# State-space scales as 128 short rows, context scales kept on chip, biases as rows, and a second product buffer, in a decoder layer on one core

## The chip, the cores and the metric

The kernel runs on one core of a Trainium2 chip. The metric is device time in microseconds (us). Engines are named as in the profile: PE is TensorE's matmuls and PEld its weight loads, DVE is VectorE, ACT is ScalarE, POOL is GpSimd, SP is SyncE, and SPq its queue. Here SP issues all DMAs. L187 is line 187 of the kernel before.

## What is computed

The reference is one decoder layer on x (16 batches, 256 positions, 512 channels) with a context tensor of the same shape. Three sublayers each add to x:

```
x = x + attention(layernorm(x))                        # 16 heads of 32, causal
x = x + state_space(ctx, ctx, layernorm(x), kernel, D) # see below
x = x + ffn(layernorm(x))                              # int8-like rounding of x, h and both weights

# state_space: 32 heads; k = v = ctx, read as (batch, 256 rows, 512)
kv[i,j] = k[i] * v[j]                  # 8 x 8 products a head
y[i,j]  = causal convolution of kv[i,j] with the head's 512-tap kernel, plus D * kv[i,j]
out[j]  = sum over i of y[i,j] * q[i]
```

The ffn rounds rows to 127 steps of their largest magnitude, does silu(gate) * up, rounds again and multiplies by the down weights.

## The kernel before

It has two long stages. In the first (0 to about 694 us) attention runs over 64 units, each a batch and a group of four heads: `project` (q and k), `scores`, `flip` and `weigh` (weights times values), with `norm`, `turn`, `values` and `project_out` once a batch. The result x1 goes to device memory, `x1_d`.

Beside attention the first stage prepares the two later sublayers:

- `pairs` (L679) makes the 8 x 8 products of the context for each of 64 pieces (2 halves of the batches, 4 groups, 8 heads). `pairs_load` (L650) loads four context tiles `ct` and computes a power-of-two scale for each row in `sm`: its column 2 goes into the context, and its column 3 (L660) is stored in device memory, `rs_d` (L661), to undo it later. `pairs_turn` scales and transposes a tile to `kT`. `pairs` itself multiplies on POOL into a float32 tile `p` (L688, L692), copies it as f16 on ACT (L696), subtracts that copy from `p` on POOL for the f16 remainder (L697) and stores both parts in `kv_d` (L698). `p` has one buffer (L685), `kv` two.
- `state_space` (L701) scales the 32 convolution kernels by powers of two, stores the 32 inverse scales in `sg_d` (L713) and padded taps in `pad_d`.
- `wjob` and the weight functions behind it round the ffn weights to `w1_d` and `w2_d`, and their scales to `sw_d`.

`pairs` is spread over units 0 to 53 of the 64 (L858). Weight jobs are `pinned` (L789): on each engine they are tied behind the newest marked instruction, among them L697 and L698.

After unit 59, `side` is closed, the pools of `pairs` and the weights with it, and `conv_open` (L123) opens the convolution's tiles. It loads `sgt`, the scales as the convolution needs them: rows 0 to 63 hold the 16 scales of even heads and rows 64 to 127 those of odd ones (L128). Then come the first three `conv_load` (L176). Each loads a tile of 128 rows of x1 (`bx`, L178), every fourth also loads four row scales `rs` from `rs_d` (L181); row norms follow (L170 on ACT, L172 on DVE, L173 on POOL), then the factor of norm, row scale and kernel scale (L185, which needs `rs` and `sgt`), the scaled query (L187), its transposes on PE (L191) and copies (L192, L193). `conv_taps` loads the products `bkv` and the taps `T`.

The second stage runs over 32 tiles: `conv` multiplies taps and products on PE into `c` (L219 to L221), weighs with the query on DVE (L224 to L230), sums on POOL and DVE (L234 to L242); `conv_out` transposes back and adds x1, with `rs` as a factor (L250); the ffn follows some tiles later (`ffn_x`, `ffn_g`, `ffn_u`, `ffn_h`, `ffn_d`). `ffn_weights` loads its weights during the first tiles.

At the very start `bias_load` (L411) loads three bias vectors of 512 so that element 128c + p stands in row p, column c, four bytes at a time (L414), and takes their largest magnitude per row (L415), which `weight_scales` needs (L428).

Two things set the order of instructions on each engine. Each engine runs its own in order. That order is not the code's: when the kernel is built a planner (L921) lays the instructions out by its own model of times, starting what it believes ready, as far as data, free buffers and `pinned` allow. The code's order is a priority.

Of the kernel before, what the change touches and what calls it, by code (L numbers as in the profile page):

```python
# [8 lines left out]
F32 = mybir.dt.float32  # L9
# [3 lines left out]
I32 = mybir.dt.int32  # L13
AF = mybir.ActivationFunctionType
ALU = mybir.AluOpType
# [19 lines left out]
def kernel(  # L35
# [4 lines left out]
    nc = tc.nc  # L40
# [5 lines left out]
    CH = ssm.shape[0]  # L46
    HB = 8
    NHF = NB // HB
    NCG = 4
    NKV = 288  # L50

    P = 128
    KC = D // P
# [3 lines left out]
    cst = ctx.enter_context(tc.tile_pool(name="cst", bufs=1))  # L57

    def dtile(shape, dt, name):
        return dram.tile(shape, dt, tag=name, name=name)  # L60
# [2 lines left out]
    DX = D + 16  # L63
    x1_d = [dtile([HB, S, DX], F32, f"x1_d{f}") for f in range(NHF)]
    kv_d = [[dtile([P, 4, 2, NKV], F16, f"kv_d{f}_{h}") for h in range(CH)] for f in range(NHF)]
    rs_d = [[dtile([P, 4], F32, f"rs_d{f}_{c}") for c in range(NCG)] for f in range(NHF)]
    pad_d = dtile([CH, 2, 640], F16, "pad_d")
    sg_d = dtile([CH, 1], F32, "sg_d")
    NG, NW = 2 * I // P, 2 * I // P + D // P
# [5 lines left out]
    idf = cst.tile([P, P], F32, name="idf")  # L75
# [18 lines left out]
    def sd(nm):  # L94
        return ps_sd.tile([P, 512], F32, tag="sd", name=f"sd_{nm}")
# [14 lines left out]


    NK = 4 * NCG
    UW = 5 * 64 + 3 * 88
    cv = ff = tail = ps_c = ps_x = sgt = vs = sw1 = sw2 = w1 = w2 = None
    us = []
# [7 lines left out]
    def conv_open():  # L123
        nonlocal cv, sgt, vs
        cv = cv_ctx.enter_context(tc.tile_pool(name="cv", bufs=2, side="right", reuse_waits="tile"))
        sgt = cv.tile([P, NK], F32, bufs=1, name="sgt")
        for j in range(2):
            nc.sync.dma_start(  # L128
                sgt[64 * j:64 * j + 64, :], bass.AP(sg_d.tensor, sg_d.offset + j, [[0, 64], [2, NK], [1, 1]]))
        for j in range(2):  # L130
            products(cv)
        vs = cv.tile([P, 4, 88], F32, bufs=1, name="vsum")
# [28 lines left out]
            return ps_av.tile([P, 512], F32, tag="av", name=nm)  # L161
        return ps_pj.tile([P, 512], F32, tag="pj", name=nm)

    x1s, x2s, qTs, oTs, rss, kvT = {}, {}, {}, {}, {}, {}
    fst = {}


# [8 lines left out]
    def conv_load(f, k):  # L176
        x1 = cv.tile([P, DX], F32, tag="x1", bufs=5, name=f"bx1_{f}_{k}")
        nc.sync.dma_start(x1[:, :D + 1], rows(x1_d[f], 0, k, D + 1, DX))  # L178
        if k % 4 == 0:
            rss[f, k // 4] = cv.tile([P, 4], F32, tag="rs", bufs=3, name=f"rs{f}_{k}")  # L180
            nc.sync.dma_start(rss[f, k // 4], rs_d[f][k // 4])  # L181
        rs = rss[f, k // 4][:, k % 4:k % 4 + 1]
        q = cv.tile([P, D], F32, tag="q", bufs=2, name=f"bq{f}_{k}")
        st = row_norm(x1, q, f"b{f}_{k}")
        nc.vector.tensor_scalar(st[:, 2:3], st[:, 2:3], rs, sgt[:, k:k + 1], ALU.mult, ALU.mult)  # L185
        nc.vector.tensor_scalar(st[:, 3:4], x1[:, D:D + 1], st[:, 2:3], -1.0 / D, ALU.mult, ALU.mult)
        nc.scalar.activation(q, x1[:, :D], AF.Identity, bias=st[:, 3:4], scale=st[:, 2:3])  # L187
        qT = cv.tile([P, 2, 4, 96], F32, tag="qT", bufs=4, name=f"qT{f}_{k}")
        pt = sd(f"q{f}_{k}")
        for li in range(4):  # L190
            nc.tensor.transpose(pt[:, li * P:(li + 1) * P], q[:, li * P:(li + 1) * P], idf)  # L191
        nc.scalar.copy(ap(qT, 0, [[96, 4], [384, 2], [1, 64]]), pt.rearrange("p (l h i) -> p l h i", l=4, h=2))  # L192
        nc.scalar.copy(ap(qT, 64, [[96, 8], [1, 32]]), ap(qT, 0, [[96, 8], [1, 32]]))  # L193
        x1s[f, k], qTs[f, k] = x1, qT
# [47 lines left out]
            nc.vector.tensor_tensor(oT[:, :, 64 * h:64 * h + 64], a, vs[:, :, 0:64], ALU.add)  # L242

    def conv_out(f, k):
        x1, rs, oT = x1s[f, k], rss[f, k // 4][:, k % 4:k % 4 + 1], oTs[f, k]
        pt = sd(f"o{f}_{k}")
        for li in range(4):
            nc.tensor.transpose(pt[:, li * P:(li + 1) * P], oT[:, li, :], idf)
        x2 = ff.tile([P, DX], F32, tag="x2", bufs=DN + 4, name=f"x2_{f}_{k}")
        nc.vector.scalar_tensor_tensor(x2[:, :D], pt, rs, x1[:, :D], ALU.mult, ALU.add,  # L250
                                       accum_out=x2[:, D:D + 1])
        x2s[f, k] = x2

    OB, ND = 6, 2
    G, U, DN = 3, 4, 6
    end = f"{NHF - 1}_{NK - 1}"
    nt = {}
# [125 lines left out]
    with ExitStack() as ph:  # L383
# [7 lines left out]
        wld = wl_ctx.enter_context(tc.tile_pool(name="wld", bufs=1, side="right"))  # L391
# [8 lines left out]
        bias = wp.tile([P, 4, KC], F32, name="bias")  # L400
# [9 lines left out]

        def bias_load():  # L411
            nc.vector.memset(bias[:, 3, :], 0.0)
            for j, src in enumerate((q_b, k_b, v_b)):
                nc.sync.dma_start(bias[:, j, :], src.rearrange("(c p) -> p c", p=P))  # L414
            nc.vector.tensor_reduce(tbp, bias, op=ALU.max, axis=AX.X, apply_absolute_value=True)  # L415
            nc.vector.tensor_tensor(tbp, tbp, tbp, ALU.mult)

# [232 lines left out]
        def pairs_load(f, c):  # L650
            ct = kvp.tile([P, 4, D], F32, tag="ct", name=f"ct{f}_{c}")
            for k in range(4):
                nc.sync.dma_start(ct[:, k, :], rows(ctxt, f * HB, 4 * c + k))
            sm = kvp.tile([P, 4, 4], F32, tag="sm", bufs=2, name=f"sm{f}_{c}")
            nc.vector.tensor_reduce(sm[:, 0, :], ct, op=ALU.max, axis=AX.X, apply_absolute_value=True)
            nc.vector.tensor_scalar(sm[:, 0, :], sm[:, 0, :], 2.0 ** -100, None, ALU.max)
            si = sm.bitcast(I32)
            nc.vector.tensor_scalar(si[:, 1, :], si[:, 0, :], EXPMASK, None, ALU.bitwise_and)
            nc.vector.tensor_scalar(si[:, 2, :], si[:, 1, :], -1, (127 + 127 + 6) << 23, ALU.mult, ALU.add)
            nc.vector.tensor_scalar(si[:, 3, :], si[:, 1, :], 6 << 23, None, ALU.subtract)  # L660
            nc.sync.dma_start(rs_d[f][c], sm[:, 3, :])  # L661
            cts[f, c] = ct, sm

        def pairs_turn(f, c, k):
# [14 lines left out]
        def pairs(f, c, h):  # L679
                if h == 0:  # L680
                    pairs_load(f, c)
                if h % 2 == 0:
                    pairs_turn(f, c, h // 2)
                kT = kTs[f, c]
                p = kvp.tile([P, 4, NKV], F32, tag="p", bufs=1, name=f"p{f}_{c}_{h}")  # L685
                kv = kvp.tile([P, 4, 2, NKV], F16, tag="kv", bufs=2, name=f"kv{f}_{c}_{h}")
                o = (h % 2) * 384
                nc.gpsimd.tensor_tensor(  # L688
                    ap(p, 0, [[NKV, 4], [64, 4], [1, 64]]),
                    ap(kT, o, [[96, 4], [0, 4], [1, 64]]),  # L690
                    ap(kT, o, [[96, 4], [8, 4], [1, 64]]), ALU.mult)
                nc.gpsimd.tensor_tensor(  # L692
                    p[:, :, 256:NKV],
                    ap(kT, o, [[96, 4], [1, 32]]),
                    ap(kT, o + 32, [[96, 4], [1, 32]]), ALU.mult)
                nc.scalar.copy(kv[:, :, 0, :], p)  # L696
                marks["POOL"] = nc.gpsimd.tensor_tensor(kv[:, :, 1, :], p, kv[:, :, 0, :], ALU.subtract).ins  # L697
                marks["SP"] = nc.sync.dma_start(kv_d[f][8 * c + h], kv).ins  # L698


        def state_space():  # L701
            kr = ldp.tile([CH, 512], F32, tag="row", name="kr")
            kd = ldp.tile([CH, 4], F32, tag="kd", bufs=1, name="kd")
            nc.sync.dma_start(kr, ssm)
            nc.sync.dma_start(kd[:, 0:1], dskip.rearrange("(h o) -> h o", o=1))
            nc.vector.tensor_tensor(kr[:, 0:1], kr[:, 0:1], kd[:, 0:1], ALU.add)
            nc.vector.tensor_reduce(kd[:, 0:1], kr, op=ALU.max, axis=AX.X, apply_absolute_value=True)
            nc.vector.tensor_scalar(kd[:, 0:1], kd[:, 0:1], 2.0 ** -100, None, ALU.max)
            kdi = kd.bitcast(I32)
            nc.vector.tensor_scalar(kdi[:, 1:2], kdi[:, 0:1], EXPMASK, None, ALU.bitwise_and)  # L710
            nc.vector.tensor_scalar(kdi[:, 2:3], kdi[:, 1:2], -1, (127 + 127 + 14) << 23, ALU.mult, ALU.add)
            nc.vector.tensor_scalar(kdi[:, 3:4], kdi[:, 1:2], 14 << 23, None, ALU.subtract)
            nc.sync.dma_start(sg_d, kd[:, 3:4])  # L713
            nc.vector.tensor_scalar(kr, kr, kd[:, 2:3], None, ALU.mult)
            pad = ldp.tile([CH, 2, 640], F16, tag="row", name="pad")
            nc.vector.memset(pad, 0.0)
            nc.vector.tensor_copy(pad[:, 0, 127:639], kr)
            nc.vector.tensor_tensor(pad[:, 1, 127:639], kr, pad[:, 0, 127:639], ALU.subtract)
            nc.sync.dma_start(pad_d, pad)
# [206 lines left out]
```

## Time and profile before

| what | value |
|---|---|
| time, median of 3 runs (lowest to highest) | 1297.2 us (1295.33 to 1301.08) |
| the profiled execution: its time | 1293.03 us |
| its span, first to last instruction | 1290.9 us |
| mean granted TensorE clock | 0.950 of full |
| busy, share of the span | PE 87%, DVE 81%, POOL 73%, ACT 63% |

The profiled execution is 4.2 us under the median, so durations from the profile add up against 1293, and differences are then taken from 1297.2.

The page also cuts the span in 40 slices of 32 us. A digit is the busy share of a slice in tenths; PEclk is the granted clock in tenths; the last row is what the DMA engines moved:

```profile
PE   4889789998998989989993688999999899999985
...
PEclk8889889999998989989998889999999999999998
...
GB/s 237 111 143 201 178 190 212 205 207 214 173 238 183 217 187 201 253 178 206 231 178 73 377 178 161 173 155 158 160 158 176 149 157 153 177 144 161 128 70 74
```

PE is busy in nearly every slice. The two low digits in the middle (slices 22 and 23, counted from 1, 678 to 742 us) are the change from attention to convolution, and the DMA engines move only 73 GB/s in the first of them. Shares of busy time over the whole span say little about such a place, so the stage has to be looked at on its own.

### The profile page before, as it was taken

The page shows a single profiled execution, that of the slowest core. Times are in us where ns is not written, and L with a number is a line of the kernel's source. Part 1 is how long each engine was busy: PE and PEld are TensorE (multiplying, and loading weights), DVE is VectorE, ACT ScalarE, POOL GpSimd, SP SyncE. Part 2 cuts the span into 40 slices and gives each one's busy share as a digit, 9 for nine tenths or more (in the row PEclk, how much of TensorE's full clock was granted, in tenths as well). Part 3 has the DMA queues.
Part 4 walks back from the last instruction along what each step waited for, and adds up shares of the span by engine and source line. Part 5 has one row for each costly group of instructions (what it writes and reads, how often), then busy time and mean ns, then how long its engine had stood idle before and what let it go on. Part 6 is the DMA issues. An engine that isn't in the chain of part 4 may idle for free.

```text
span 1290.9 us, 25306 instructions
## 1 busy us (share of the span) xinstructions
PE 1127.8 (87%) x8487; PEld 775.5 (60%) x8487; DVE 1044.8 (81%) x3034; ACT 818.5 (63%) x1970; POOL 940.5 (73%) x882
## 2 busy tenths in 40 slices
PE   4889789998998989989993688999999899999985
PEld 3656556665666656657661465766666666666652
DVE  5778866876888698788872577999999999999984
ACT  4678766785877778778882444555555545555553
POOL 2367677776886868778772679888788788888862
PEclk8889889999998989989998889999999999999998
DMA  7556767678676876867752956665556555656433
GB/s 237 111 143 201 178 190 212 205 207 214 173 238 183 217 187 201 253 178 206 231 178 73 377 178 161 173 155 158 160 158 176 149 157 153 177 144 161 128 70 74
DMA packets 276904, 229.98 MB, mean 178 GB/s; under 512 B 133069, under 2 KB 231399, under 8 KB 276647
## 3 DMA queue, kind: packets, MB, share of 16 engines
q1 hardware_dynamic: 276775, 228.37, 63.0%
q8 instruction: 67, 1.10, 0.4%
q14 instruction: 62, 0.51, 0.1%
HBM read 124.11 MB, written 75.76 MB: 155 GB/s over the span
## 4 chain that ended last, share of the span: by engine, by line
DVE 36%; PE 23%; DMA 19%; POOL 7%; ACT 6%; issue 5%; SPq 4%; ACTq 0%; DVEq 0%; POOLq 0%
DMA bx<-x_d 6%; DVE u L224 3%; DVE oT L242 3%; DVE g L302 3%; DVE p L573 3%; DMA xt<-in_x_dram 3%; DVE u L227 3%; DMA ct<-in_ctx_dram 2%; PE pj_qk L473 2%; PE pj_qk L474 2%; PE pj_qk L475 2%; DVE hp L321 2%; ACT p L577 2%; DVE s L323 1%; PE s L568 1%
## 5 line engine op out<-in xcount | busy, mean ns | idle before, releaser
L577 ACT ACTIVATE p<-p,nmax 128x128 f32<-128x128 f32 (+1 forms) x512 | 227.9, 449 | 65.5 <-DVE nmax L573 64.4
L697 POOL TENSOR_TENSOR kv<-p,kv 128x1152 f16<-128x1152 f32 x64 | 152.1, 2377 | 91.0 <-ACT kv L696 90.6
L573 DVE CUSTOM_DVE_ANT_0 p<-s,mask,esc 128x128 f32<-128x128 f32 (+1 forms) x512 | 186.8, 410 | 36.5 <-PE s L568 36.0
L219 PE MATMUL c<-bkv,T 128*128 128x288 f16 x640 | 185.4, 290 | 13.3 <-DVE u L230 4.6
L221 PE MATMUL c<-bkv,T 128*128 128x288 f16 x640 | 185.1, 289 | 0.0
L220 PE MATMUL c<-bkv,T 128*128 128x288 f16 x640 | 185.1, 289 | 0.0
L688 POOL TENSOR_TENSOR p<-kT 128x1024 f32<-128x1024 f32 x64 | 144.4, 2257 | 0.9
L238 POOL TENSOR_TENSOR u<-u 128x512 f32<-128x512 f32 x64 | 82.6, 1291 | 46.8 <-DVE u L224 46.6
L568 PE MATMUL s<-st 96*128 96x128 f16 (+1 forms) x512 | 80.4, 254 | 24.6 <-DVE nmax L573 18.0
L305 POOL TENSOR_TENSOR g<-g,sw 128x1408 f32<-128x1408 f32 x30 | 96.2, 3206 | 3.8 <-ACT g L304 3.8
L577 ACT ACTIVATION_READ_ACCUMULATOR p<-p,nmax 128x1 f32 x512 | 98.4, 192 | 0.0
L300 PE MATMUL g<-w,xq 128*128 128x384 bf16 x496 | 89.0, 313 | 9.3 <-DMA xq<-xb 4.2
L318 PE MATMUL u<-w,xq 128*128 128x384 bf16 x496 | 89.3, 316 | 5.4 <-DVE g L302 2.5
L353 PE MATMUL d<-w,hq 128*128 128x512 bf16 x341 | 80.7, 385 | 13.9 <-DMA hq<-hb 9.6
L224 DVE TENSOR_TENSOR u<-c,qT 128x512 f32<-128x512 f32 x128 | 87.2, 681 | 4.9 <-PE c L221 4.6
L219 PEld LDWEIGHTS <-T 128*128 128x128 f16 x640 | 63.3, 99 | 40.3 <-issue 11.0
L170 ACT ACTIVATE bq<-bx 128x512 f32<-128x512 f32 x32 | 23.1, 721 | 96.4 <-DMA bx<-x_d 96.2
L533 ACT ACTIVATE qkhl<-pj_qk,bias 128x256 f16<-128x256 f32 x128 | 59.6, 468 | 33.1 <-DVE qkhl L534 23.1
L473 PE MATMUL pj_qk<-xhT,wq_hi 128*128 128x256 f16 x256 | 71.0, 278 | 8.8 <-DMA xhT<-xh 6.8
L234 POOL TENSOR_TENSOR vsum<-u 128x352 f32<-128x352 f32 x64 | 59.9, 937 | 22.8 <-DVE oT L242 11.5
L568 PEld LDWEIGHTS <-st 96*128 96x128 f16 x512 | 47.8, 101 | 47.7 <-issue 31.1
L474 PE MATMUL pj_qk<-xlT,wq_hi 128*128 128x256 f16 x256 | 71.0, 277 | 5.4 <-DMA xlT<-xl 5.3
(218 smaller groups left out, 3597.7 us busy)
## 6 DMA issues: line engine op xcount, KB each, us to landing
kv_d<-kv SPq DMA_DIRECT2D x64, 576.0 KB, 3.3
bkv<-kv_d SPq DMA_DIRECT2D x64, 576.0 KB, 4.2
qk_d<-qkhl SPq DMA_DIRECT2D x64, 256.0 KB, 2.9
st<-qk_d SPq DMA_DIRECT2D x256, 64.0 KB, 2.5
T<-pad_d SPq DMA_DIRECT2D x64, 256.0 KB, 4.4
x_d<-xt SPq DMA_DIRECT2D x32, 256.5 KB, 2.5
bx<-x_d SPq DMA_DIRECT2D x32, 256.5 KB, 4.3
xt<-in_x_dram SPq DMA_DIRECT2D x16, 512.0 KB, 4.8
```

Source lines behind the costliest of these rows:

```text
L219: nc.tensor.matmul(reg, T[:, 0, d:d + P], kv[:, mi, 0, :], start=mi == 0, stop=False)
L220: nc.tensor.matmul(reg, T[:, 0, d:d + P], kv[:, mi, 1, :], start=False, stop=False)
L221: nc.tensor.matmul(reg, T[:, 1, d:d + P], kv[:, mi, 0, :], start=False, stop=mi == li)
L224: nc.vector.tensor_tensor(ap(u, uo, [[UW, 2], [64, 4], [1, 64]]), ap(pc, 0, [[512, 2], [64, 4], [1, 64]]), ap(qT, qo, [[96, 2], [8, 4], [1 ...
L305: (nc.gpsimd if (f, k) not in tiles[-ND:] else nc.vector).tensor_tensor(g1[:, c], g1[:, c], sw1[:, I + c.start:I + c.stop], ALU.mult)
L473: nc.tensor.matmul(ps, lh, rh, start=first, stop=False)
L474: nc.tensor.matmul(ps, lh, rl, start=False, stop=False)
L568: nc.tensor.matmul(ps[:, hh, :nk], stk[:, 0, h, qc * P:(qc + 1) * P], stk[:, 1, h, :nk], start=True, stop=True)
L573: marks["DVE"] = nc.vector.tensor_tensor_reduce(out=pr[:, h, :], in0=ps[:, hh, :nk], in1=mk, op0=ALU.add, op1=ALU.min, scale=esc[:, 0:1], ...
L577: marks["ACT"] = nc.scalar.activation(pr[:, h, :], pr[:, h, :], AF.Exp, scale=-1.0, bias=nmax[:, qc, h:h + 1], accum_out=lsum[:, qc, h:h + ...
L688: nc.gpsimd.tensor_tensor(ap(p, 0, [[NKV, 4], [64, 4], [1, 64]]), ap(kT, o, [[96, 4], [0, 4], [1, 64]]), ap(kT, o, [[96, 4], [8, 4], [1, 6 ...
L697: marks["POOL"] = nc.gpsimd.tensor_tensor(kv[:, :, 1, :], p, kv[:, :, 0, :], ALU.subtract).ins
```

## The change

The scales' way to the convolution is new. `state_space` stores `sg_d` as before and then loads all 32 scales into each of 128 rows (`sgall`); `conv_open` picks even and odd ones with two copies on DVE. The context's row scales are written into a tile that stays in on-chip memory (`rsall`), and the store and loads through `rs_d` go. The biases are loaded as 12 rows of 128 numbers and turned with one PE transpose and a DVE copy. The float32 product tile `p` gets two buffers.

```diff
-    rs_d = [[dtile([P, 4], F32, f"rs_d{f}_{c}") for c in range(NCG)] for f in range(NHF)]
...
+    rsall = cst.tile([P, NHF, NK], F32, name="rsall")
+    sgall = cst.tile([P, CH], F32, name="sgall")
...
         for j in range(2):
-            nc.sync.dma_start(
-                sgt[64 * j:64 * j + 64, :], bass.AP(sg_d.tensor, sg_d.offset + j, [[0, 64], [2, NK], [1, 1]]))
+            nc.vector.tensor_copy(
+                sgt[64 * j:64 * j + 64, :], sgall[64 * j:64 * j + 64, :].rearrange("p (k j) -> p j k", j=2)[:, j, :])
...
-        if k % 4 == 0:
-            rss[f, k // 4] = cv.tile([P, 4], F32, tag="rs", bufs=3, name=f"rs{f}_{k}")
-            nc.sync.dma_start(rss[f, k // 4], rs_d[f][k // 4])
-        rs = rss[f, k // 4][:, k % 4:k % 4 + 1]
+        rs = rsall[:, f, k:k + 1]
...
-        x1, rs, oT = x1s[f, k], rss[f, k // 4][:, k % 4:k % 4 + 1], oTs[f, k]
+        x1, rs, oT = x1s[f, k], rsall[:, f, k:k + 1], oTs[f, k]
...
             nc.vector.memset(bias[:, 3, :], 0.0)
+            brow = wld.tile([3 * KC, P], F32, name="brow")
             for j, src in enumerate((q_b, k_b, v_b)):
-                nc.sync.dma_start(bias[:, j, :], src.rearrange("(c p) -> p c", p=P))
+                nc.sync.dma_start(brow[KC * j:KC * j + KC, :], src.rearrange("(c p) -> c p", p=P))
+            pt = sd("bias")
+            nc.tensor.transpose(pt[:, :3 * KC], brow, idf[:3 * KC, :3 * KC])
+            nc.vector.tensor_copy(bias[:, 0:3, :].rearrange("p j c -> p (j c)"), pt[:, :3 * KC])
...
-            nc.vector.tensor_scalar(si[:, 3, :], si[:, 1, :], 6 << 23, None, ALU.subtract)
-            nc.sync.dma_start(rs_d[f][c], sm[:, 3, :])
+            nc.vector.tensor_scalar(rsall.bitcast(I32)[:, f, 4 * c:4 * c + 4], si[:, 1, :], 6 << 23, None, ALU.subtract)
...
-                p = kvp.tile([P, 4, NKV], F32, tag="p", bufs=1, name=f"p{f}_{c}_{h}")
+                p = kvp.tile([P, 4, NKV], F32, tag="p", bufs=2, name=f"p{f}_{c}_{h}")
...
             nc.sync.dma_start(sg_d, kd[:, 3:4])
+            nc.sync.dma_start(sgall, bass.AP(sg_d.tensor, sg_d.offset, [[0, P], [1, CH]]))
```

More of the change, by code (lines that the diff above doesn't have):

```diff
@@ L162, in acc @@
         return ps_pj.tile([P, 512], F32, tag="pj", name=nm)
-    x1s, x2s, qTs, oTs, rss, kvT = {}, {}, {}, {}, {}, {}
+    x1s, x2s, qTs, oTs, kvT = {}, {}, {}, {}, {}
     fst = {}
```

## The prediction

> **What bounds the kernel now.** I read the page first, then the list of waits, then the queue of SP, two-microsecond windows and engine timelines around the longest waits. The list of waits (engine, line, what it waited for: us in total, times, longest us) has two single waits of some 20 us and one wait that comes 48 times:
>
> ```profile
> ACT bq L170 <- DMA bx<-x_d: 96.2, 25, 19.2
> POOL kv L697 <- ACT kv L696: 90.6, 48, 5.6
> ...
> PE sd_q L191 <- ACT bq L187: 21.2, 1, 21.2
> ```
>
> The two long ones are one hole, between attention and convolution: TensorE ends attention at 694.2 and starts on the first transposes of the convolution's query (L191) at 715.4, because ScalarE (L170) waits for the first `bx`. SP's queue shows why that load is late (start us, us, what):
>
> ```profile
> 686.68 0.96 SPq L774 DMA_DIRECT2D sw_d<-swt  x1
> 687.68 1.62 SPq L128 DMA_DIRECT2D sgt<-sg_d  x2
> 689.35 3.19 SPq L178 DMA_DIRECT2D bx<-x_d  x1
> 692.58 6.73 SPq L181 DMA_DIRECT2D rs<-rs_d  x1
> ```
>
> The two `sgt` loads go in just ahead of `bx`. They are 4 KB each and the slowest loads of the case; an ordinary `bx` takes 4.3 us (last column: median us to landing):
>
> ```profile
> bx<-x_d SPq DMA_DIRECT2D x32, 256.5 KB, 4.3
> ...
> sgt<-sg_d SPq DMA_DIRECT2D x2, 4.0 KB, 17.4
> ```
>
> Windows of 2 us (last three columns: TensorE's granted clock, DMA share, GB/s) say what the DMA engines do meanwhile:
>
> ```profile
> 696.00:698.00 2.00, 0.00 (x0) 0.00 (x0) 0.00 (x0) 0.00 (x0) 0.00 (x0) 1.00 0.05 0
> 700.00:702.00 2.00, 0.00 (x0) 0.00 (x0) 0.00 (x0) 0.00 (x0) 0.00 (x0) 0.50 0.05 0
> 710.00:712.00 2.00, 0.00 (x0) 0.00 (x0) 0.00 (x0) 0.07 (x1) 0.00 (x0) 0.50 1.06 299
> ```
>
> From 690 to 708 a share of 0.05, about one engine in sixteen, and 0 GB/s: one DMA engine works off 4-byte pieces. Two loads of 64 rows by 16 numbers are 2,048 pieces; over the 19 or so us that is 9.3 ns a piece. Everything behind waits. The chain of waits says it too: 22.51 us at `bx`.
>
> **Part 1: `sgt` loads become one early load and two copies.** Gone: both L128 loads. `bx` is then issued where L128 was, at 687.68, and lands after its usual 4.3 us at 692.0. ScalarE ends attention (L631) at 692.69, so L170 starts at 692.7 instead of 711.93: **19.2 us** earlier. The steps behind are as before (711.93 to 715.38: norm, scale, transposes), so TensorE resumes at 696.2, its first convolution product (716.29 before) at 697.1. Are its other inputs there? From 686.2 on, kv_d 0.59, w_d 0.36, three `bx` 0.79, `bkv` 0.59 and `T` 0.26 MB go out: 2.6 MB at the 384 GB/s seen at 714 to 716 take 6.7 us, to 692.9, and some 2 us to land. Yes. The hole shrinks to 2 us, so the clock stays: before, it was 0.50 from about 699 to 719, twelve products came at 0.24 instead of 0.122 us apart (1.4 us), the transposes took 1.11 instead of 0.60 (0.5 us). Another **1.9 us**.
>
> Here a rule of the Trainium skill speaks against me. "DMA: Bandwidth & Descriptors", section "Why a DMA increments its semaphore by 16 and not by 1", has a transfer split over the largest number of engines up to 16 that divides both sides' outermost sizes; 64 rows would use all 16. Then 2,048 pieces take 2,048/16 x 9.3 ns = 1.2 us, and removing them wins about 1 us. The 0.05 row says one engine, so I take 19.2. For the new load, 128 rows of 128 B, it matters little: even on one engine 128 pieces x 9.3 ns = 1.2 us, near the `rs` load's 4.4 us in all.
>
> Its place does matter. It stands behind `sg_d` (issued at 75.91, landing 3.0 us later) and must wait for it, with `pad_d`, one kv_d, one qk_d and three `ct` loads behind it on SP. Bounds: 0 if the planner puts these ahead, 3 us if all slide and TensorE misses a score load. SP's next score loads (L541) start at 84.3 anyway, after 4 us without an issue. I take 0.
>
> The two copies on VectorE (64x16) are new: near 0.15 us (L656's least). The page "SBUF — State Buffer", section "SBUF: two separate sides", has VectorE and GpSimd share one port pair as an exclusive lock, the loser blocked for the whole instruction. This bears out here and is dearer than a row's minimum:
>
> ```profile
> L659 DVE TENSOR_SCALAR sm<-sm x8: 151/1376/2284, 34.2 to 555.1; 128x4 int32<-128x4 int32 x8
> ```
>
> A four-column operation takes from 151 to 2,284 ns, the length of a GpSimd product. By the least row the copies cost 0.3, by the rule up to 2 x 2.4 = 4.8 us. VectorE has nothing from 694.8 to 712.8, and the copies can run before; I take 0.
>
> **Part 2: context scales stay on chip.** Gone: 8 stores `rs_d` and 8 loads `rs`: 8 x 0.35 + 8 x 0.58 = 7.4 us of SP's issuing, none of it waited for except behind `sgt`. L660 writes the same 4 columns elsewhere. L185 and L250 now read what VectorE itself wrote. Worth 0 (the other bound is 8 x 0.58 = 4.6 us, if each load held back a `bx` that is waited for).
>
> **Part 3: biases as rows.** Three loads of 4 rows of 512 B replace three of 512 pieces; added are one transpose on TensorE (0.27, L431's row), a copy (0.15, L441's), and TensorE's wait for the rows. Behind that wait are the weights' transposes, which wait until 8.14 for `wl_q`. L415 moves from 4.27 to perhaps 5; its reader L428 runs at 13.54. Cost 0; `wl_q` may land up to 0.5 us earlier.
>
> **Part 4: two buffers for the products.** No instruction is added or removed. GpSimd runs in order, and its order is laid down by the planner when the kernel is built. The planner does not keep to the text: TensorE turns a piece of `wo` at 25.09, ahead of the first projection product at 26.94, though the code has it after four projections. With one `p`, the next L688 can't stand ahead of L697, which reads `p`; so GpSimd idles 90.6 us in front of L697. Each pair is a chain of 2.25 (L688) + 0.46 (L692) + 1.14 on ScalarE + 2.38 (L697) plus waits; the 64 L688 go from 66.7 to 678.9, one each 9.7 us, though the code spreads the 64 heads over 54 of the 64 units. A unit takes 10.0 us (the 64 weighings' L618 run from 58.0 to 690.1), so by the code they would be done near 600. On GpSimd's timeline the last one is
>
> ```profile
> 683.44 2.37 POOL L697 TENSOR_TENSOR kv<-p,kv 128x1152 f16<-128x1152 f32 x1 [0.26 <-ACT kv L696]
> ```
>
> and the chain of waits (start us, us, what) hands it on at once to SP:
>
> ```profile
> 683.44 2.38 POOL kv L697
> 685.84 0.32 SPq L698
> 686.21 0.42 SPq L767
> 686.68 0.96 SPq L774
> ```
>
> With a second `p` the planner can put L688 into that idle time. The pairs then end tens of us earlier, and with them the last kv_d and the w_d and sw_d stores that are tied behind it; the convolution's loads go out while attention still runs, and TensorE can take convolution products from 685.7, when L606 frees the last of the score banks that they reuse. Between there and 694.2 attention fills TensorE 6.1 us (18 output products 0.216 apart, 3.9, and two weighings of 1.1), so 2.5 us lie open, and 2.9 more up to 697.1: 5.4 us to fill. I count **4**, since norm and output steps hold VectorE and ScalarE there too. What is late next is the fill of the convolution itself: TensorE's 7.4 us wait at 738 for `oT` remains. I give attention itself no gain: no GpSimd result is among the waits of TensorE from 60 to 690.
>
> **Sum.** 19.2 + 1.9 + 4 = 25.1. The profiled execution took 1293.0 (span 1290.9), giving 1267.9; the median shown, 1297.2, lies 4.2 above it, giving **1272.1, say 1272**. Half a per cent is 6.5 us.
>
> **The rivals.**
> - *Transition only*: the planner leaves the pairs late; their ScalarE copies still stand behind the exponentials (L577). 21.1 us: 1276. For: only free choices of the planner move the pairs. Against: its free hand elsewhere. Chance 0.32; the forecast has 0.42.
> - *More*: the pairs' copies and products out of the way also shorten TensorE's waits in attention (18 us on L573), and the fill at 738 overlaps: 35 to 40 us, 1260. For: POOL and ACT lighter in the last stretch; against: VectorE, full there, gets no lighter. 0.08.
> - *Hidden anyway*: loads all come together, `bkv` and `T` land 10 us late (12.7 and 12.1 at worst before) and hold the products: gain 11, 1286. Against: the bytes above. 0.06.
> - *The change doesn't do it*: the scale path still sits before `bx`, or new order costs what is won: 1297. 0.04.
> - *Slower*: the planner puts a product (L688 + L692, 2.7 us) in front of `lb` (L584) or `xl` (L503), and in-order TensorE waits for them in attention. In one of four units: 16 x 2.7 = 43, less 21: 1319. It decides against the change from 8 units on (21.1/2.7). For: GpSimd idles 35.8 us in front of `lb`, just where a planner will fill. Against: `lb` is used a unit (10 us) later. 0.08.
>
> So faster 0.88, same 0.04, slower 0.08. The range, 1259 to 1286, takes the two main cases with about 5 us of reshuffled order around, the larger gain and the half-hidden one.
>
> **What would show it.** Right: no 4-byte crawl at 690 to 708; TensorE's gap at the transition under 5 us, clock not at 0.50; `bx` near 4.3 us; L697's wait for L696 well under 90 us and the last L697 before 660; convolution products among attention's last. Only part 1: last L697 still near 685, gap 2 to 3 us. Wrong: TensorE waiting for GpSimd in 60 to 690, or the stretch from first to last convolution product (716 to 1232) longer than 516 us.

## The result, and the profile after

The changed kernel takes **1295.6 us** (median of 12 runs, 1288.7 to 1300.4) against 1297.5 for the kernel before in the same series (12 runs, 1293.0 to 1301.1). The ratio is 0.999, 95% interval 0.9972 to 1.0008: no change. The forecast was 1272, in a range of 1259 to 1286. The profiled execution of the changed kernel has a span of 1294.1 us (1290.9 before).

Lines of the changed kernel are named as its own profile has them; L697 of before is L699 here, L696 is L698, L170 is L172, L503 (`xl`) is L506. In E4, E5, E11, E12 and E14 to E16 below, the lines of attention and pairs are one higher than before (L697 is L698).

The page's slices (busy tenths of TensorE, granted clock in tenths):

```profile
PE   5889988888988889899989978999999999999974
...
PEclk9899998899989999999989989999999999999988
...
```

TensorE's slices 22 and 23, 3 and 6 before, are 9 and 9 now, at a clock of 9 and 9 where it was 8 and 8. The list of waits of the whole span (us in total, times, longest):

```profile
ACT bq L172 <- DMA bx<-x_d: 69.6, 26, 5.7
...
POOL kv L699 <- ACT kv L698: 42.9, 28, 4.1
```

The single wait of 19.2 us for `bx` is gone, the one of 21.2 us for the scaled query with it, and the subtraction's wait has halved from 90.6 us. SP's queue (start, us, what) shows the convolution's loads while attention still runs:

```profile
639.68 1.87 SPq L180 DMA_DIRECT2D bx<-x_d  x3
641.60 0.60 SPq L198 DMA_DIRECT2D bkv<-kv_d  x1
```

and on TensorE the first convolution products come among attention's last output products and weighings, without a hole:

```profile
710.24 0.38 PE L477 MATMUL pj_o<-wo_lo,ah 128*128 128x512 f16 x1
710.93 0.28 PE L218 MATMUL c<-bkv,T 128*128 128x288 f16 x1 [0.31 <-DVE t L609]
```

So what the change was to do at the transition it does. But attention is late: its last output product on TensorE, which ended at 694.2 before, now ends at 724.7, with convolution products between the last ones. How the delay grows shows in a step that each of the 64 weighings has once, VectorE's product `av<-av,lt` (L630 before, L633 now). Its starts, with the units counted from 0:

| weighing of unit | 0 | 28 | 52 | 60 | last (63) |
|---|---|---|---|---|---|
| before, us | 65.0 | 358.9 | 605.8 | 678.3 | 691.7 |
| changed, us | 65.7 | 377.5 | 622.0 | 701.8 | 719.8 |

From the last of these to the end of the span the kernel before takes 599.2 us and the changed one 574.3. That is 24.9 us won behind attention, near the 25.1 of the forecast. But the last itself comes 28.1 us later.

Windows (busy us of TensorE, weight loads, VectorE, ScalarE and GpSimd with their counts, clock, DMA share, GB/s) say the same of the stretch from 200 to 600 us. Before, and then changed:

```profile
200.00:400.00 200.00, 180.31 (x1456) 124.70 (x1454) 154.25 (x524) 148.65 (x456) 149.69 (x119) 0.94 0.75 209
400.00:600.00 200.00, 186.00 (x1498) 127.20 (x1496) 161.29 (x528) 152.90 (x463) 151.40 (x120) 0.95 0.74 207
```

```profile
200.00:400.00 200.00, 175.35 (x1360) 119.06 (x1354) 160.82 (x491) 145.22 (x430) 165.12 (x132) 0.91 0.75 209
400.00:600.00 200.00, 178.10 (x1478) 123.51 (x1476) 152.51 (x523) 156.00 (x460) 166.63 (x129) 0.97 0.78 222
```

TensorE has 116 instructions fewer on record in these 400 us (2,954 to 2,838), GpSimd is 31 us busier: the pairs, whose last subtraction started at 683 before, are done by 584 (start of the last L699).

### The profile page after: what moved, and what is told of

Its sections match the earlier page's. It is cut to its first block, busy times and chain, and to the rows that moved or that the text cites. A ratio compares the mean times of both kernels' runs of the same rounds, so it can differ in the third digit from the quotient of the medians.

```text
span 1294.1 us, 25324 instructions
## 1 busy us (share of the span) xinstructions
PE 1137.3 (88%) x8488; PEld 779.9 (60%) x8488; DVE 1041.0 (80%) x3037; ACT 815.5 (63%) x1970; POOL 940.2 (73%) x882
## 4 chain that ended last, share of the span: by engine, by line
DVE 35%; DMA 23%; PE 17%; POOL 8%; ACT 7%; issue 6%; SPq 3%; DVEq 0%; POOLq 0%; ACTq 0%
DMA bx<-x_d 6%; DMA xt<-in_x_dram 4%; DVE u L223 3%; DVE g L301 3%; DVE u L226 3%; DVE p L576 3%; DVE oT L241 3%; ACT p L580 2%; DMA xlT<-xl 2%; DVE hp L320 2%; SPq L544 2%; DVE o L361 2%; DMA ct<-in_ctx_dram 2%; DMA qk_d<-qkhl 1%; POOL p L690 1%
## 5 line engine op out<-in xcount | busy, mean ns | idle before, releaser
L699 POOL TENSOR_TENSOR kv<-p,kv 128x1152 f16<-128x1152 f32 x64 | 152.6, 2388 | 43.1 <-ACT kv L698 42.9
L587 POOL TENSOR_SCALAR lb<-lsum 128x256 f32<-128x256 f32 x64 | 26.5, 414 | 114.3 <-DVE lsum L586 70.8
L317 PE MATMUL u<-w,xq 128*128 128x384 bf16 x496 | 92.4, 316 | 1.7 <-DVE hp L320 1.3
L537 DVE SCALAR_TENSOR_TENSOR qkhl<-pj_qk,bias,qkhl 128x256 f16<-128x256 f32 x128 | 60.4, 475 | 34.8 <-ACT qkhl L536 34.5
L600 PE MATMUL pt<-idf,p 128*128 128x128 f32 x256 | 69.1, 293 | 14.5 <-DVE t L605 9.1
```

The lines of the kernel that those rows point to most:

```text
L317: nc.tensor.matmul(pg[:, :n].rearrange("p (r o) -> p r o", o=P), xq[:, kc, :], w1[:, (I + c.start) // P:(I + c.stop) // P, kc, :], start=k ...
```

## The experiments

Three theories. **A**: the second product buffer lets the planner pack the products early and densely, and attention beside them gets slower. **B**: the planner redraws the order of all engines when an edit shifts its model of times; the parts of the change cost nothing, the new order does. **C**: the context scales on chip, or memory places, cost by themselves. Ratios are to the kernel before on the same chip, and differences between runs of different chips are taken from the ratios (1% is 13 us); "last" is the start of the last weighing's `av<-av,lt` in the profiled execution (before: 691.7).

| run | what | us | ratio, 95% | last |
|---|---|---|---|---|
| E1 | changed, one product buffer | 1284.2 | 0.9945 (0.9919 to 0.9971) | 710.0 |
| E2 | before, two buffers | 1304.6 | 1.0101 (1.0062 to 1.014) | 733.0 |
| E3 | before, bias rows | 1291.6 | 0.9989 (0.9971 to 1.0006) | 690.9 |
| E4 | before, scales early | 1270.0 | 0.9832 (0.98 to 0.9863) | 694.0 |
| E5 | E4, two buffers | 1283.7 | 0.9908 (0.9877 to 0.9939) | 710.4 |
| E6 | E5, products tied | 1289.8 | 0.9964 (0.9939 to 0.9989) | 718.0 |
| E7 | changed, loads held | 1282.2 | 0.989 (0.986 to 0.9921) | 710.4 |
| E8 | E4, context scales on chip | 1291.4 | 0.9965 (0.9944 to 0.9985) | 711.3 |
| E9 | changed, E4's order | 1270.5 | 0.9825 (0.9799 to 0.9851) | 694.2 |
| E10 | E8, E4's order | 1270.5 | 0.9806 (0.9776 to 0.9836) | 693.4 |
| E11 | E5, E4's order, 12 products moved | 1271.1 | 0.9818 (0.9796 to 0.984) | 692.9 |
| E12 | as E11, 29 moved | 1275.3 | 0.986 (0.9821 to 0.99) | 701.5 |
| E13 | E9, pairs free | 1283.0 | 0.9891 (0.9876 to 0.9905) | 711.7 |
| E14 | E4, eight memsets at unit 3 | 1289.9 | 0.9934 (0.9908 to 0.9959) | 718.8 |
| E15 | E4, eight memsets at unit 6 | 1291.1 | 0.9957 (0.9934 to 0.998) | 707.9 |
| E16 | E14, two buffers | 1311.2 | 1.0096 (1.0064 to 1.0128) | 729.7 |
| E17 | changed, own order, loads held | 1284.9 | 0.9946 (0.9926 to 0.9967) | 706.2 |

### The parts one by one (E1 to E4)

E1 is the changed kernel with `bufs=1` for `p`; E2, E3 and E4 are the kernel before with one part alone: `bufs=2`, the bias rows, or the early scales (`sgall` and the two copies).

E1: 

> The change with one product buffer instead of two. Theory A (the second buffer squeezes the products into less time, attention beside them runs slower, and that gives back what the transition won): attention ends near 694 us as before, the hole in TensorE at the transition shrinks from 21 to 2-3 us, and the time is near 1276 us (ratio 0.984). Rival B (the planner lays out a new order at every edit, and attention comes out some 20 us longer or shorter whatever the edit): attention ends anywhere, and the ratio can be 0.97 to 1.01. Rival C (scales on chip or the early convolution loads slow attention): attention ends near 715 to 720 as in the change, ratio near 1.0.

E2: 

> The kernel before with two product buffers, nothing else. Theory A: the products end near 590 us, attention's units run 20 to 30 us late by unit 48, and the slow scale loads now fall into attention, where they hold up SP's queue for 18 us: ratio 1.005 to 1.02. Rival B: no set direction. Rival C: attention as before, and the pairs' early end lets the slow loads hide: ratio 0.98.

E3: 

> The kernel before with only the biases loaded as rows. Theories A and C: ratio 1.000 within 0.003, attention ends near 694 us. Rival B: the order is new from early on, so attention may come out 5 to 20 us different, ratio 0.985 to 1.015.

E4: 

> The kernel before with only the state-space scales loaded early as 128 rows (two copies at the convolution's opening). Theory A: the hole at the transition shrinks to about 3 us, attention as before, ratio 0.984. Rival B: the hole shrinks, attention anywhere. Rival C: attention ends later, ratio near 1.0.

E4 alone wins 1.7%, more than any of the others and all that the forecast gave to it. TensorE's timeline in E4:

```profile
695.94 0.59 PE L476 MATMUL pj_o<-wo_hi,al 128*128 128x512 f16 x2
697.00 0.66 PE L192 MATMUL sd_q<-idf,bq 128*128 128x128 f32 x4 [0.47 <-ACT bq L188]
699.20 0.30 PE L220 MATMUL c<-bkv,T 128*128 128x288 f16 x1 [1.53 <-DMA T<-pad_d]
```

The transposes follow attention after 0.5 us, where 21 us lay open. The second buffer alone loses 1%, and with it the subtraction's last start falls from 683 to 592 while the last weighing goes to 733. That spoke for A. But E1, with one buffer, lies 14 us above E4 and has its last weighing at 710. A has no explanation for that, so B and C were still in.

How far an order was redrawn can be counted: match the instructions of two profiles by engine, operation, tile names and occurrence, and count how many at least must have changed places. On TensorE up to 600 us, none of 4,177 has between the kernel before, E3 and E4. Against E4, 815 of 4,128 have in E1, 1,252 of 4,039 in E2 and 1,239 of 4,074 in the changed kernel. The two edits that left the order alone, E3 and E4, are also the two whose times came as theory A and the forecast had them.

### Pairs of parts (E5 to E8)

E5 is E4 with `bufs=2`; E8 is E4 with `rsall`. E6 is E5 with each product tied to the pair before, so that the second buffer can't be used:

```diff
+                    if "POOL" in marks:
+                        es.enter_context(tc.issue_after(marks["POOL"]))
                     nc.gpsimd.tensor_tensor(
```

E7 is the changed kernel with the convolution's early loads tied behind attention's last load of scores:

```diff
+                with tc.issue_after(last["st"]):
                     at(conv_load, 0)
...
                     taps(1)
```

E5: 

> The kernel before with two parts of the change alone: the early load of all scales with two copies, and two buffers for the products. It differs from the changed kernel by the context scales on chip and the bias rows only. Theory A (the second buffer lets the planner pack the products, attention beside them runs late): attention's last weighing 20 to 40 us after E4's 694.0, no hole at the transition, pairs end by 600, ratio 0.995 to 1.005 to before, some 1295 us. Rival B (any edit redraws the planner's order, no part has a price of its own): anywhere from 1270 to 1305, with attention's end not tied to where the pairs end. Rival C (the context scales on chip are what slows attention): about 1270, last weighing near 694.

E6: 

> As E5, with both product buffers in memory, but each product is tied behind the subtraction of the pair before it, as one buffer would force. Theory A: the squeeze cannot happen, so pairs end near 683 as in E4, last weighing within 4 us of 694, ratio 0.980 to 0.988, some 1272 us. Rival B: the tie is one more edit, so the time may lie anywhere from 1270 to 1305. A third reading, that the second buffer costs by its memory alone: as E5.

E7: 

> The changed kernel with the convolution's early loads (three loads of x1 and two of taps and products) tied behind attention's last load of scores. Theory A with its second part (3.8 MB of early loads stand ahead of attention's score loads at 640 to 660 us): TensorE's 4-us wait at 655 to 660 and the clock of 0.73 at 660 to 670 go, the last weighing comes 5 to 10 us before the changed kernel's 719.8, the convolution starts no later than there, ratio 0.990 to 0.995. If those loads only show the lateness and do not cause it: last weighing within 3 us of 719.8, ratio 0.997 to 1.001. If the convolution needs them that early: slower than before.

E8: 

> The kernel before with the early load of all scales and with the context scales kept on chip; one product buffer, old bias loads. It lies between E4 (1270.0) and E1 (1284.2, which has the bias rows too). Rival C (keeping the context scales on chip slows attention, through VectorE's write into a tile that lives on or the order it brings): last weighing near E1's 710, ratio 0.990 to 0.997, some 1284 us. Theory A alone (only the second buffer costs): last weighing within 4 us of 694, ratio 0.980 to 0.986, some 1270 us, and then E1's 14 us belong to the planner's order with the bias rows.

E6 was to give E4's time by A and gave 1290. E8 differs from E4 by the tile that L660 writes and by sixteen DMAs of 2 KB (E4 has no long wait for the eight loads among them), and it too takes 1291. Against E4 each of E5, E6 and E8 lost 10 to 17 us by the ratios, whatever its edit was. That is B's picture, or C's for E8; E7's gain couldn't be read, since its order differs from the changed kernel's from 640 us on. An edit that shuffles all five engines can't price a part. The order had to be held.

### The order held (E9 to E12)

The place of every instruction on its engine in E4 was written down as a list, and each instruction tied to the one before it on its engine, without a wait (`ORDER` is the packed list; what the change alone has, such as the bias transpose, is left free):

```diff
+    for one in zlib.decompress(base64.b85decode(ORDER)).decode().split(";"):
+        at, prev = 0, None
+        for step in one.split(","):
+            at += int(step)
+            if prev is not None:
+                tc.add_manual_dep(ins[at], prev.name, nosync, reason="replay")
+            prev = ins[at]
```

E9 is the whole change, E10 is E8, each in E4's order. In E11 the list has 12 products (L688, L692 of before) ahead of the subtraction (L697) that stood directly before them, in E12 29 of them, 17 of which also pass one to three other GpSimd operations.

E9: 

> The whole change, all four parts, with each engine's instructions held in the order that the planner gave to E4 (list of places, one tie from each instruction to the next on its engine); the bias transpose and its copy, which E4 has not, are left free. Theory B (the change's parts cost nothing by themselves; what is lost is the planner's new order): as E4, last weighing within 4 us of 694, pairs end near 685, 1266 to 1275 us, ratio 0.978 to 0.986. Theory A (the second buffer's order is bad because products are packed): the same figure, since no packing can happen in this order. Theory C (memory places, the context scales on chip, or the bias rows cost by themselves): 1280 to 1295 as in E1, E8 and the changed kernel.

E10: 

> E8 (scales early, context scales on chip, one product buffer) held in E4's order on each engine. E8 took 1291.4, E4 1270.0; they differ by eight stores and eight loads of 2 KB. Theory B (order alone): 1266 to 1275 us, last weighing within 4 us of 694. Theory C (the tile that lives on costs by itself): 1285 to 1295.

E11: 

> E5's kernel (scales early, two product buffers) in E4's order, with one edit: the 12 products that in E4 follow directly on the subtraction of the pair before go ahead of it, into GpSimd's wait for ScalarE. This is what the second buffer was forecast to do, without any other new order. GpSimd gains up to 12 times 2 us of waiting; nothing is put ahead of `lb` or `xl`. If GpSimd's idle time in front of the subtraction is worth nothing to attention, as the forecast had it: within 3 us of E4's 1270, wait of the subtraction 15 to 25 us less. If a lighter GpSimd helps: 1262 to 1267. If any moved product delays attention: above 1274.

E12: 

> As E11, with 29 products moved ahead of the subtraction of the pair before, the 12 of E11 and 17 that also pass one to three other operations of GpSimd (`lb`, `xl`, the residual's bias, context scaling), each of which then waits some 2.7 us longer. Theory A (products ahead of `lb` and `xl` are what makes attention late): each passed `lb` or `xl` that TensorE or VectorE waits for costs up to 2.7 us, together 10 to 40 us, last weighing 704 or later. If these operations have slack, as the forecast's main case has it: within 4 us of E11.

**E9 is the answer to what the change's parts cost in a held order: nothing.** With all four parts it takes 1270.5 us, by the ratios 21 less than the same code in the planner's own order, and E10 takes 21 less than E8. Up to 600 us none of TensorE's 4,177 instructions stands elsewhere than in E4, in either. C falls. TensorE in E9, 200 to 600 us:

```profile
200.00:400.00 200.00, 178.80 (x1449) 123.17 (x1448) 154.47 (x525) 148.26 (x454) 148.43 (x119) 0.94 0.73 206
400.00:600.00 200.00, 186.98 (x1517) 128.11 (x1516) 161.53 (x532) 154.48 (x469) 153.46 (x123) 0.96 0.76 211
```

2,966 TensorE instructions, as before (2,954). In E11 the moved products do fill waits. GpSimd's waits from 60 to 690 us, E4 and then E11:

```profile
POOL kv L698 <- ACT kv L697: 90.6, 48, 5.4
POOL lb L585 <- DVE lsum L584: 37.8, 21, 7.6
```

```profile
POOL kv L698 <- ACT kv L697: 79.4, 42, 5.4
POOL lb L585 <- DVE lsum L584: 46.8, 24, 8.3
```

11 us leave the first row, and 9 appear in the second: GpSimd just waits elsewhere, and the time is E9's within the interval. E12's 17 passings, ten of them of `lb` and one of `xl`, cost 4 us against E11 by the medians (the intervals overlap), some 0.25 us each and not 2.7: `lb` mostly has slack. For `xl` one passing says little.

### What makes an order slow (E13 to E17)

E13 is E9 with the pairs' own instructions left out of the list. E14 and E15 redraw E4's order with work that has nothing to do with the change (at unit 3, or 6); E16 is E14 with `bufs=2`:

```diff
+            if u == 3:
+                with tc.issue_after(marks["DVE"]):
+                    idle = cst.tile([P, 32], F32, name="idle")
+                    for k in range(8):
+                        nc.vector.memset(idle, float(k))
```

E17 is E7's tie again, with the changed kernel's own list for attention, pairs and weights.

E13: 

> The whole change with all instructions held in E4's order as in E9, but for those of the pairs (context loads, scales, transposes, products, casts, subtractions, stores), which the planner may put where it likes. With two product buffers it ends them at unit 46 of 64, earlier than in the changed kernel (unit 50), and GpSimd's order differs from E4's accordingly; attention's own order is E4's. Theory A (early, dense products slow attention): last weighing 704 or later, ratio 0.988 to 1.0. Theory B (the redrawn order of attention costs, not the pairs): last weighing within 5 us of 694, ratio 0.977 to 0.985, 1265 to 1276 us; if early pairs bring what part 4 of the forecast had, 4 us below E9.

E14: 

> E4 (one product buffer) with eight memsets of 128x32 on VectorE, under 1 us of work together, tied behind the newest scores when unit 3 is written down. They serve nothing; they shift the planner's model a little, and attention's order comes out as different from E4's as that of the changed kernel. Theory B: 8 to 25 us slower than E4, 1278 to 1295, last weighing 702 or later. Theory A: within 5 us of E4's 1270.

E15: 

> As E14, with the eight memsets at unit 6: another redraw of E4's order. Theory B: 1278 to 1295. Theory A: within 5 us of E4's 1270.

E16: 

> As E14 with two product buffers, so a redraw of E5 (1283.7). Theory B: in the same spread as E14 and E15, 1278 to 1295. Theory A: at least 10 us slower than E14 and E15.

E17: 

> The changed kernel with attention, pairs and weights held in the changed kernel's own order on every engine, and the convolution's first loads (three of x1, two of taps and products) tied behind attention's last load of scores; all else of the convolution is left to the planner. If the early loads ahead of attention's score loads cost what E7 won: within 4 us of E7's 1282, last weighing 706 to 714, no 4-us wait for scores at 655 to 660. If E7 won by its redraw of attention: within 4 us of the changed kernel's 1295.6.

**Eight memsets of 0.085 us each cost 13 and 16 us** against E4 by the ratios (E14, E15), with one buffer and no other part: B holds. On TensorE up to 600 us, 1,040 of 4,067 and 918 of 4,125 instructions stand elsewhere than in E4. E14's windows and its largest TensorE waits from 60 to 690 us:

```profile
200.00:400.00 200.00, 170.86 (x1374) 117.32 (x1373) 149.79 (x494) 141.15 (x430) 147.47 (x118) 0.96 0.73 196
400.00:600.00 200.00, 173.96 (x1459) 120.34 (x1456) 154.98 (x521) 149.56 (x455) 149.46 (x121) 0.98 0.73 206
```

```profile
PE s L569 <- DMA st<-qk_d: 18.7, 10, 3.9
PE s L569 <- DVE nmax L574: 15.4, 14, 8.2
PE pj_qk L475 <- DMA xlT<-xl: 12.4, 7, 4.8
```

The same list for E9 has 5.4 us for `st`, 20.5 for `nmax` and 5.3 for `xlT`. In E15 those three rows are 5.3, 23.2 and 4.3, as good as in E9, and it is late all the same. So none of these waits marks a slow order.

A is not empty either. In E13 attention's order is E4's (without the pairs' instructions, the profiles of E13 and E9 have one order up to 660 us) and only the pairs are early: the last subtraction starts at 548. It takes 9 us more than E9 by the ratios. While the products are dense, attention falls back: unit 28's weighing starts 27.5 us after E9's, the last one 17.5. The windows of E13:

```profile
200.00:400.00 200.00, 172.03 (x1382) 118.74 (x1381) 153.78 (x478) 145.68 (x427) 175.40 (x137) 0.91 0.72 214
...
600.00:680.00 80.00, 78.73 (x673) 54.71 (x671) 59.72 (x231) 58.97 (x199) 16.55 (x17) 1.00 0.54 148
```

GpSimd is 88% busy from 200 to 400 us (E9: 74%), and in the last line, where it is nearly free, TensorE is full with or without the pairs (673 instructions, E9 660). The early pairs slow a stage that later has little empty TensorE time to catch up in.

The profile of E13 shows two places where the dense pairs press on attention; no run prices them singly. ScalarE's copy now waits until a buffer of `kv` is stored:

```profile
ACT kv L698 <- DMA kv_d<-kv: 22.2, 14, 7.8
```

Every kernel whose pairs are packed has this wait between 60 and 690 us (5.0 to 22.2 us; the changed kernel 6.0), and none of the others has it: the second buffer of `p` moves part of the wait on to the two of `kv`, on the engine that also computes attention's exponentials. And once TensorE waits 10.3 us, at 326 us, for VectorE's `al`:

```profile
PE av L621 <- DVE al L635: 11.7, 3, 10.3
```

Ahead of `al` stand three of the pairs' scale operations on 128x4 numbers. They take 1.79, 2.04 and 2.15 us, and each ends with the GpSimd instruction beside it, as five of the eight L659 did in the kernel before. The last of the three:

```profile
323.25 2.21 POOL L690 TENSOR_TENSOR p<-kT 128x1024 f32<-128x1024 f32 x1
323.34 2.15 DVE L662 TENSOR_SCALAR sm<-sm 128x4 int32<-128x4 int32 x1
```

E16 came as A had it, 21 us slower than E14 by the ratios. In all four couples of kernels that differ by the buffer alone, the one with two is slower: E2 and before (13 us), E5 and E4 (10), E16 and E14 (21), the changed kernel and E1 (6). This speaks for a price of the second buffer beside that of the redraw. In each couple attention's order differs too, so only E13 shows it with the order held.

Last, the early loads. In the changed kernel from 650 to 670 us, and in E17:

```profile
650.00:660.00 10.00, 5.66 (x40) 3.60 (x38) 6.06 (x26) 8.74 (x31) 0.96 (x2) 0.93 0.87 226
660.00:670.00 10.00, 10.00 (x73) 6.66 (x72) 5.21 (x26) 7.22 (x25) 0.95 (x2) 0.73 0.29 95
```

```profile
650.00:660.00 10.00, 7.96 (x76) 5.95 (x74) 6.50 (x25) 6.36 (x24) 0.41 (x1) 1.00 0.01 2
660.00:670.00 10.00, 10.00 (x74) 6.22 (x75) 2.55 (x7) 3.63 (x10) 0.41 (x1) 1.00 0.47 134
```

The loads issued from 639.7 fill the DMA engines (share 1.00 from 640 to 650 us), TensorE's wait for scores behind them (`st`, one wait of 4.0 us) and a granted clock of 0.73 follow; in E17 both are gone. E17 is 0.9946 against the changed kernel's 0.999; the intervals (0.9926 to 0.9967, 0.9972 to 1.0008) do not meet, so this is worth about half a per cent, some 6 us. (E17 leaves the rest of the convolution to the planner, so a part may be its order there.) E7's further 7 us are then most likely its redraw.

Together, from E9's 0.9825 to 0.999: early loads about 6 us (E17), dense pairs about 9 (E13), and the remainder, about 6, put down to the redraw of attention's order, whose price alone was 13 and 16 in E14 and E15. The three overlap and were not measured as a sum. With two buffers redraws gave 0.9908, 0.9964, 0.999 and 1.0096 (E5, E6, changed, E16), with one 0.9934, 0.9945, 0.9957 and 0.9965 (E14, E1, E15, E8). Why the order of before, which E3 and E4 keep, beats each of these eight stays open, and so does what in a redrawn order is slow.

E4 and E9 beat both kernels; they differ by less than the intervals tell.

## Why the prediction was wrong

- **Part 1, 21.1 us: right in size, in part by luck.** E4 has 1.68%, 21.8 us of 1297. `bx` goes out at 689.1, and the transposes start 0.5 us after attention's last product. But in E4's profile the first convolution product comes 17.1 us earlier (716.29 to 699.20), not 19.2: "Are its other inputs there? Yes" missed by the 1.5 us that it waits for `T`, and attention's last weighing is 2.3 us later. Some 7 us come in the first tiles instead, the fourth of which begins 34.6 us after the first and not 41.9: the wait for `oT` that part 4 let remain went from 7.4 to 2.7 us. The 1 us that the prediction worked out from a split over 16 engines did not come. Four-byte pieces are not slow in themselves: before, each bias load is 512 such pieces and lands in 2.2 to 2.4 us, while the two `sgt` loads of 1,024 took 12.7 and 22.1. Why those crawl was not tested. In the changed kernel the early load landed after 5.1 us, and the two copies took 0.35 us together. No GpSimd instruction ran beside them, so the 4.8 us of a shared port was not put to the test.
- **Parts 2 and 3, nothing: right** as costs of their own. E10 and E4 don't differ, E3 is null.
- **Part 4, 4 us: wrong.** The pairs ended early, the wait of L697 halved, and the convolution's first products came among attention's last, as forecast. But filling the wait in front of L697 is worth nothing (E11), and pairs placed as freely as the second buffer allows cost 9 us (E13). The loads that go out "while attention still runs" take the DMA engines from it (E17).
- **The step that failed**: "I give attention itself no gain: no GpSimd result is among the waits of TensorE from 60 to 690." I took this for no loss too, and took attention's order as given while only the pairs moved; the range had "about 5 us of reshuffled order". The planner laid out all five engines anew. The runs show a loss of 21 us in place of that nothing (E9 against the changed kernel), and by E14 and E15 a redraw alone can cost 13 to 16. I had even shown its free hand (the turn of `wo` at 25.09), and read it only as a chance.
- **The rivals.** "New order costs what is won: 1297" is what happened, at a chance of 0.04. So its end was named, with next to no weight. "Slower", with products ahead of `lb` and `xl` at 2.7 us in each unit, is not what the traces show: in the changed kernel a product stands directly ahead of `xl` 5 times (3 before) and of `lb` 17 times (15 before). TensorE's waits for `xlT` from 60 to 600 us did grow, by 7 us (the first line is before, the second changed), and E12 prices a passing at some 0.25 us:

```profile
PE pj_qk L474 <- DMA xlT<-xl: 4.0, 2, 3.5
```

```profile
PE pj_qk L477 <- DMA xlT<-xl: 11.3, 8, 3.8
```

Neither of the prediction's two signs of being wrong came. TensorE's waits for GpSimd from 60 to 690 us in the changed kernel are one of 0.8 us, and the stretch from first to last convolution product is 515.9 us long. Both watch one cause or the stage behind attention; a table of attention's unit starts, as above, would have shown the loss by unit 28.

## What to carry to other kernels

Where a planner sets the order, a change has two prices: that of its instructions and buffers, which the profile of before can tell in part, and that of the new order, which it can't; here the first was −23 us (E9) and the second +21. Price a part with the order held, and if the part is good, keep the old order with it. A freed buffer lets work run early. Here that was worth nothing where it filled GpSimd's waits (E11), and it cost time where it crowded the engines that attention needed (E13).

## What the runs showed of the hardware beyond that

The changed kernel and E17 have the same instructions in the same order on all engines up to some 640 us, yet in the profiled executions the weighing of unit 52 starts at 622.0 in one and 611.2 in the other. The granted clock from 200 to 400 us is 0.91 in the changed kernel (shown above) and 0.96 in E17:

```profile
200.00:400.00 200.00, 173.90 (x1396) 118.22 (x1394) 164.40 (x507) 149.74 (x443) 171.98 (x137) 0.96 0.77 220
```

E17's profiled execution took 1276.9 us, 8 under its median. Profiles of E4's order lie closer together: in those of before, E3, E4, E9, E10 and E11 unit 52 starts between 603.8 and 607.3. In a redrawn order a difference of 10 us between two profiles is thus not read as an effect here; the verdicts rest on the medians and their intervals.
